# Two states to a GpSimd product, rotating pair buffers and a new table of sum slots in a selective-scan kernel

## The chip, the cores and the metric

The kernel runs on one core of a Trainium2 chip, in one launch. The metric is the device time of that launch in microseconds (us), as the median of several runs. A core has TensorE (PE, matrix products into PSUM), VectorE (DVE), ScalarE (ACT), GpSimd (POOL) and SyncE (SP, which here only issues DMA transfers). Each engine works through its own instructions in order.

## The reference, cut to what matters

The input is x of shape 16 x 192 x 64 x 64. Four layers follow each other, each of the form `x = x + layer(_gn(x))`, where `_gn` is a group norm with 32 groups. Layer 0 is a small network per channel with tanh and sigmoid, layer 1 a 1x1 convolution over five shifts of the image, layer 3 a sum of depthwise convolutions, a 1x1 convolution and a batch norm over all images. The change lies in layer 2, a selective scan in four directions k (rows, columns, and both backwards), with 16 states for each channel:

```python
def step(h, inp):
    d, u, Bt, Ct = inp
    dA = jnp.exp(d[..., None] * A)
    h = dA * h + (d * u)[..., None] * Bt[:, :, None, :]
    y = jnp.einsum('bkdn,bkn->bkd', h, Ct)
    return (h, y)
...
ys = jnp.moveaxis(ys, 0, -1) + xs * Ds.reshape(K, D)[None, :, :, None]
```

The outputs of the four directions are added in image order, and the residual adds the layer's input to that.

## The kernel before, in words

Two images are taken together: 2 x 192 channels are three tiles j of 128 partitions, and there are eight such pairs. `front` holds layers 0 and 1, the projection that gives B, C and the step sizes (`project`), and a transposition for the column directions (`split`). `scans` holds layer 2, `layer3` the last layer. The front of pair 0 runs alone; then, for each pair, `scans` runs with the front of the next pair woven in, and `layer3` follows. The last pair's `scans` has no front to weave in. The batch norm at the end closes the kernel.

In `scans` the work is 48 steps t for a pair: three tiles j, four directions k in the order 1, 3, 0, 2, and four pieces of the sequence of LC = 1024 elements. Each step has 16 states n, so there are 768 iterations s for a pair. The order of instructions on each engine is the one in which the program issues them (`E.in_order`); no scheduler changes it. One iteration s issues:

- `load_c(s+2)`: SP loads the C row of that state to all partitions (`cb`, four buffers).
- `product(s)`: DVE multiplies `du` (delta times the input) by B, in place in PSUM (`pbt`).
- `scan(s)`: DVE runs the recurrence into a buffer `h` (pool `hp`, eight buffers of LC); ACT copies the last state; POOL multiplies h by `cb`. For n = 1, 5, 9, 13, POOL also issues a transfer that adds the h of state n-1 into that of n, so of four states three are left to sum.
- `decay(s+3)`: ACT makes dA = exp(delta A).
- `spread(s+2)`: PE spreads B over the partitions with a bf16 product into one of two PSUM buffers `pbt`.
- Front work of the next pair. A credit of one unit an iteration (none at n = 5) is spent on it. A yield of layer 0 costs one unit and holds up to four 512-column f32 matmuls; a matmul of layer 1 or of the projection costs 0.57.
- `add_up(s-4)`: PE adds the h of four iterations ago to `ysum` by an identity matrix. In the places of n = 0, 4, 8, 12 `images` adds other inputs instead: for k = 0 the raw input `xc`, the normalised input through a diagonal matrix `skip`, and the sum of the column directions `Xt`; for k = 3 and k = 2 what the earlier direction left. After state 15 ACT copies ysum out.

`step_rest` makes delta and du of the next step: its matmul v (which shares the PSUM buffer of ysum) is issued at n = 4, the POOL product du at n = 10. The iteration of n = 3 issues its sum, the last of the previous step, ahead of the front work; all the others issue it behind. In layer 0, `x_rows` has SP copy the rows of a unit to the tile `m0`, ACT and PE make `t1` and `t2` from it, and `close` of the next unit adds t2 to the result. A unit is 32 rows of one chunk; a pair has 96 of them.

In the profile all instructions that `E` orders carry line L66, so they are told apart by the names of their tiles.

Of the kernel before, what the change touches and what calls it, by code (L numbers as in the profile page):

```python
# [43 lines left out]
LATE = 4  # L44
# [8 lines left out]
GAP = 25  # L53
# [53 lines left out]
def conv_preact_kernel(ctx: ExitStack, tc: tile.TileContext, a: dict):  # L107
# [43 lines left out]
    dtw = const.tile([32 + RD, K, NT, P], F32, name="t_dtw")  # L151
    for r in (0, 32):
        nc.sync.dma_start(out=dtw[r : r + RD], in_=a["dtw"])
# [11 lines left out]
    skip = const.tile([P, NT, P], F32, name="skip")  # L165
# [11 lines left out]
    for j in range(NT):  # L177
        nc.vector.tensor_scalar(skip[:, j, :], ident, dsk[:, 0, j : j + 1], None, ALU.mult)
# [126 lines left out]
    class Made:  # L305
        def __init__(self, n):
            def d(name, shape, dtype=F32):
                return dram.tile(shape, dtype, name=f"{name}{n}")

            self.x2 = d("x2_d", [NT * P, L])  # L310
            self.b = d("b_d", [P, L])
            self.c = d("c_d", [P, L])
            self.dt = d("dt_d", [K * RD, L])

            self.bp = d("bp_d", [K, BP, L], BF16)
            self.cp = d("cp_d", [2 * 2 * N, L])
            self.dtp = d("dtp_d", [2 * RD, L])
            self.gm = const.tile([P, NT], F32, name=f"gm{n}")
            self.rstd = const.tile([P, NT], F32, name=f"rstd{n}")

# [38 lines left out]
    def group_norm(E, st, stat, ps, gm, rstd, tiles=range(NT)):  # L359
# [50 lines left out]
        E.gps.tensor_tensor(rstd, d2, half, ALU.pow)  # L410


    def front(i, o, E, ps, deep):

        with tc.tile_pool(name="f_st", bufs=1) as stat:
            sts = [stat.tile([P, NT, 8, 6], F32, name=f"fst{n}") for n in range(3)]
# [35 lines left out]
            yield from layer1(o, E, ps, deep, sts[2], gms[1], rstds[1])  # L452
            yield from group_norm(E, sts[2], stat, ps, o.gm, o.rstd)
# [4 lines left out]
    def layer0(i, E, ps, deep, st, gm, rstd):  # L458
        with tc.tile_pool(name="l0w", bufs=1) as w_, tc.tile_pool(name="l0x", bufs=3) as xk, tc.tile_pool(
# [11 lines left out]
            def stream(chunks, no):  # L471
# [116 lines left out]
                for u, (ci, q) in enumerate(units):  # L588
# [13 lines left out]
                    t2 = tk.tile([GR, 2, 512], F32, name="t2", tag=f"t2{no}")  # L602
# [37 lines left out]
    def layer1(o, E, ps, deep, st, gm, rstd):  # L640
        with tc.tile_pool(name="l1w", bufs=1) as w_, tc.tile_pool(name="l1x", bufs=2) as xk, tc.tile_pool(
            name="l1r", bufs=6
# [24 lines left out]
            def load_r(c):  # L667
                if c < 8:
                    for j in range(NT):
                        xrs[c, j] = rk.tile([P, 512], F32, name="l1_xr")  # L670
                        E.sp.dma_start(
                            out=xrs[c, j], in_=row_tiles(x1_d)[:, j, 512 * c : 512 * c + 512]
                        )
# [23 lines left out]
            load_r(0)  # L697
# [4 lines left out]
            for c in range(8):  # L702
                at = 0
                for jo in range(NT):
                    p = ps("l1_p")
                    n, last = 0, 5 * len(INTO[jo]) - 1
                    for b, ji in INTO[jo]:
                        for s, (dy, dx) in enumerate(((0, 0), (0, 1), (0, -1), (1, 0), (-1, 0))):
                            E.pe.matmul(
                                p,  # L710
                                w1[:, b, s, :],
                                xps[c][:, ji, 1 + dy : 9 + dy, 1 + dx : 65 + dx],
                                start=(n == 0),
                                stop=(n == last),
                            )
                            n += 1
                            at += 1
                            if at == 4:
                                load(c + 1)
                            if at == 8:  # L720
                                load_r(c + 1)
                            if at in (15, 20, 25):
                                norm(c + 1, at // 5 - 3)
                            yield 0.57
                            advance()
                    after.append(done(c, jo, p))
# [5 lines left out]
    def project(o, E, ps):  # L732

        with tc.tile_pool(name="pjw", bufs=1) as w_, tc.tile_pool(name="pjx", bufs=3) as xk:
# [21 lines left out]
            def done(to, c, m, p):  # L756
# [4 lines left out]
                E.sp.dma_start(out=to[:, 512 * c : 512 * c + 512], in_=r)  # L761
# [34 lines left out]
    def split(o, E):  # L796

        with tc.tile_pool(name="sp1", bufs=1) as one, tc.tile_pool(name="sp2", bufs=2) as two:
            nat = one.tile([P, L], F32, name="nat")
            E.sp.dma_start(out=nat[0:64, :], in_=o.b[0:64, :])  # L800
            E.sp.dma_start(out=nat[64:128, :], in_=o.c[0:64, :])
# [19 lines left out]
            for m in range(NC_):  # L821
# [3 lines left out]
                ct = two.tile([P, LC], F32, name="ct")  # L825
# [3 lines left out]
                E.sp.dma_start(out=o.cp[:, cs], in_=ct[64:128, :])  # L829
# [23 lines left out]

    def load_dt(sp, o, k, at):
# [9 lines left out]
    def make_delta(E, v, delta, dt, k, j):  # L864

        for h in range(2):
            rows = slice(32 * h, 32 * h + RD)
            E.pe.matmul(
                v[:, 512 * h : 512 * h + 512], dtw[rows, k, j, :], dt[rows, :], start=True, stop=True
            )  # L870
# [3 lines left out]
    def load_first(o):  # L874
# [6 lines left out]
        return xn, load_bp(nc.sync, o, k, 0), dt  # L881

    def begin(o, loaded, psum):
# [3 lines left out]
        xn, bp, dt = loaded  # L887
        normalise(nc.vector, xn, xn, o.gm, o.rstd, 0)
        delta = over.tile([P, LC], F32, name="delta", tag="delta", bufs=2)
        make_delta(E, psum(), delta, dt, k, 0)  # L890
        du = over.tile([P, LC], F32, name="du", tag="du", bufs=2)
        nc.gpsimd.tensor_tensor(image(du), image(delta), columns(xn)[:, : LC // HW, :], ALU.mult)
        return xn, bp, delta, du

    def scans(i, o, p3, st3, begun, nxt):

        E = _Engines(tc, True)
        with ExitStack() as es:
# [5 lines left out]
            hp = pool("l2h", 8)  # L904
            da = pool("l2a", 3)
            cp = pool("l2c", 4)
# [5 lines left out]
            Xt = one.tile([P, L], F32, name="Xt")  # L912

# [7 lines left out]
            xns, xcs, state, bps, dts, made, ysum = {}, {}, {}, {}, {}, {}, {}  # L921
# [13 lines left out]
            def next_dt(t):  # L935
                if t < T:
                    j, k, at, first = todo[t]
                    dts[t] = load_dt(E.sp, o, k, at)

# [13 lines left out]
            def load_xc(t):  # L953
                if t < T and todo[t][1] == 0:
                    j, k, at, first = todo[t]
                    xcs[t] = one.tile([P, LC], F32, name="xc")
                    E.sp.dma_start(out=xcs[t], in_=row_tiles(o.x2)[:, j, at : at + LC])

            def load_c(s):
                t, n = divmod(s, N)  # L960
                j, k, at, first = todo[t]
                cb = cbs[s] = cp.tile([P, LC], F32, name="cb")
                src, row = (o.c, 64 + 16 * k) if k % 2 == 0 else (o.cp, 16 * (k - 1))
                for b, rows in {
# [4 lines left out]
                    r = row + N * b + n  # L969
                    E.sp.dma_start(  # L970
                        out=cb[rows, :],
                        in_=src[r : r + 1, at : at + LC].to_broadcast([rows.stop - rows.start, LC]),
                    )

            def step_rest(t):
# [5 lines left out]
                make_delta(E, v, delta, dts.pop(t), k, j)  # L981
# [28 lines left out]
            def scan(s):  # L1010
# [4 lines left out]
                dA, pbt, cb = dAs.pop(s), pbs.pop(s), cbs.pop(s)  # L1015
                back = k >= 2
                flip = slice(None, None, -1) if back else slice(None)
                h = hs[s] = hp.tile([P, LC], F32, name="h")
# [5 lines left out]
                E.gps.tensor_tensor(h, h, cb, ALU.mult)  # L1024
                if n % 4 == 1:
                    E.gps.dma_start(out=h, in_=hs[s - 1], accum_op=ALU.add)

            def add_up(s):

                t, n = divmod(s, N)  # L1030
                if s < 0:
                    return
                j, k, at, first = todo[t]
                if n % 4 == 0:
                    for c in range(LC // 512):
                        for w, v in images(t, n // 4 - 1, 512 * c):
                            E.pe.matmul(
                                ysum[t][:, 512 * c : 512 * c + 512], w, v, start=False, stop=False
                            )
                    return  # L1040
                h = hs.pop(s)
                if n % 4 == 1:
                    hs.pop(s - 1)
                if n == 1:
                    ysum[t] = py.tile([P, LC], F32, name="ysum", tag="ysum")
                for c in range(LC // 512):
                    cs = slice(512 * c, 512 * c + 512)
                    E.pe.matmul(
                        ysum[t][:, cs], ident, h[:, cs], start=(n == 1), stop=(n == N - 1)
                    )  # L1050
                if n == N - 1:
                    if k % 2:
                        E.act.copy(Xt[:, at : at + LC], ysum.pop(t))
                    else:
                        E.act.copy(rows_of(at, LC), image(ysum.pop(t)))

            def images(t, which, c):
# [3 lines left out]
                if k == 0:  # L1061
                    of = [
                        (ident, lambda: xcs[t][:, c : c + 512]),
# [9 lines left out]
                return [(w, v()) for w, v in of[which : which + 1]] if which >= 0 else []  # L1073
# [10 lines left out]
            xns[0], bps[0], *made[0] = begun  # L1084
            next_dt(1)
            for s in range(3):
                decay(s)
            for s in range(2):
                load_c(s)
                spread(s)  # L1090
            fr = front(*nxt, E, ps, False) if nxt is not None else iter(())
# [11 lines left out]
            for s in range(total):  # L1103
                t, n = divmod(s, N)
                j, k, at, first = todo[t]
                if s + 2 < total:
                    load_c(s + 2)
                if n == 2:
                    next_bp(t + 1)
                if n == 4:  # L1110
                    next_dt(t + 2)
                if n == 11:
                    load_xc(t + 1)
# [5 lines left out]
                if n == 4:  # L1119
# [8 lines left out]
                if (t + 1) % (K * NC_) == 0 and 5 <= n < 5 + NC_:  # L1128
                    norm_xn(j + 1, n - 5)
                if n > 4:  # L1130
# [3 lines left out]
                if n == 3:  # L1134
                    add_up(s - LATE)
                    if s >= LATE and todo[t - 1][1] == ORDER[-1]:
                        fin = finish(todo[t - 1][0], todo[t - 1][2] // LC)
                elif n == 10:
                    next(gstep, None)

                credit = min(credit, 0) + (n != 5)
# [3 lines left out]
                if n != 3:  # L1145
                    add_up(s - LATE)
            for s in range(total - LATE, total):
# [9 lines left out]
    def layer3(i, st3, less0, rstd0, o_next):  # L1157
        E = _Engines(tc, False)

        with tc.tile_pool(name="l3s", bufs=1) as stat, tc.tile_pool(name="l3z", bufs=2) as zk, tc.tile_pool(  # L1160
# [5 lines left out]
        ) as pz:  # L1166
            gap.tile([P, GAP * 256], F32, name="gap")
            diag = xk.tile([P, NT, PE_TAPS, P], F32, name="diag")
            xps = [xk.tile([P, S, S], F32, name=f"xp{j}") for j in range(NT - 1)] + [X]
# [278 lines left out]
```

## Time and profile before

| | |
|---|---|
| median of the runs | 27446.29 us (27440.91 to 27455.52, three runs) |
| the profiled execution | 27459.08 us, span 27457.3 us |
| mean granted TensorE clock | 0.938 |
| busy share of the span | PE 85%, DVE 87%, ACT 59%, POOL 75% |
| scans of pair 0, with a front woven in | 1202.7 to 4114.7 us: 2912.0 us |
| scans of the last pair, without a front | 23979.2 to 26746.3 us: 2767.1 us |
| layer 3 of pair 0 | 4114.7 to 4455.0 us: 340.3 us |
| C loads | 8192 DMA issues, 512 KB for each full row block |
| POOL products h*C | 6144, 2465 ns each |
| accumulating transfers | 1536, 7.4 us from issue to landing |

The span is the time from the first to the last instruction of the profiled execution. In the tables of the profile, "x" ahead of a number is a count, "idle before" is how long the engine stood idle ahead of an instruction, and the name behind "<-" is what released it. A matmul of f32 with 512 columns runs as two passes, so the records of "x4" in a timeline are two matmuls.

### The profile page before, as it was taken

Reading aid. Unit: us, or ns where it says so; the run is one execution under the profiler, and the core shown is the slowest. Engines: PE = TensorE matmul, PEld = TensorE weight load, DVE = VectorE, ACT = ScalarE, POOL = GpSimd, SP = SyncE. Lnnn points to the kernel's source line nnn. Section 1 sums busy time; section 2 is a strip of 40 time slices with the busy share of each in tenths; the row PEclk is TensorE's granted clock in tenths of the full one; section 3 lists DMA queues with packets and bytes.
Section 4 is the critical chain, followed back from the end, with each engine's and each line's share of the span. In section 5 each row is a group of like instructions: output and inputs, shape, how many; then the busy total and the mean of one; then the engine's idle time right before and its main releaser. Section 6 shows DMA issues by size and latency. Waiting matters only on the chain. (4 is left out here: it accounts for less than half of the span.)

```text
span 27457.3 us, 209986 instructions
## 1 busy us (share of the span) xinstructions
PE 23391.4 (85%) x58036; PEld 9490.8 (35%) x58036; DVE 23876.2 (87%) x15098; ACT 16298.7 (59%) x23334; POOL 20528.5 (75%) x10322
## 2 busy tenths in 40 slices
PE   8799888998789987999879988899878998766663
PEld 4343333333333332333334333333333333222221
DVE  0399998999889998999989999899989999899994
ACT  7388555874568644785447845587456864444443
POOL 2388876888778876888768887788877887677772
PEclk9899998999899998999989999999989999888886
DMA  4489874898668974898748987489856897467765
GB/s 102 132 221 226 220 226 131 224 219 218 181 182 225 222 213 142 221 224 224 218 138 220 227 219 220 138 222 218 219 173 188 225 222 215 137 190 194 202 186 245
DMA packets 2009593, 5471.86 MB, mean 199 GB/s; under 512 B 551592, under 2 KB 551816, under 8 KB 1991008
## 3 DMA queue, kind: packets, MB, share of 16 engines
q1 hardware_dynamic: 1783776, 4592.80, 57.7%
q0 software_dynamic: 221184, 805.40, 15.4%
q10 hardware_dynamic: 3456, 60.21, 0.5%
q8 instruction: 463, 7.59, 0.1%
q14 instruction: 714, 5.85, 0.1%
HBM read 3908.47 MB, written 340.96 MB: 155 GB/s over the span
## 5 line engine op out<-in xcount | busy, mean ns | idle before, releaser
L66 POOL TENSOR_TENSOR h<-h,cb 128x1024 f32<-128x1024 f32 x6144 | 14812.9, 2465 | 4331.0 <-ACT state L66 3637.1
L66 DVE TENSOR_TENSOR_SCAN h<-dA,state,pbt 128x1024 f32<-128x1024 f32 x4608 | 10807.6, 2345 | 727.0 <-ACT dA L66 119.9
L66 PE MATMUL ysum<-h,ident 128*128 128x512 f32 x18432 | 9280.1, 628 | 171.6 <-DMA h<-h 119.1
L66 DVE TENSOR_TENSOR pbt<-du,pbt 128x1024 f32<-128x1024 f32 x6144 | 7433.2, 1210 | 569.1 <-PE pbt L66 412.6
L66 ACT ACTIVATE dA<-delta,t_alog 128x1024 f32<-128x1024 f32 x6144 | 7034.6, 1146 | 6.5
L66 PEld LDWEIGHTS ysum<-h,ident 128*128 128x128 f32 x18432 | 3692.8, 202 | 4379.4 <-issue 3858.9
L66 ACT COPY state<-h 128x1 f32<-128x1 f32 x6144 | 1143.3, 186 | 6161.7 <-DVE h L66 6143.2
L66 PE MATMUL pbt<-bp,pick 96*128 96x512 bf16 x8192 | 2623.4, 404 | 1888.0 <-DVE h L66 1867.3
L66 DVE TENSOR_TENSOR_SCAN h<-dA,pbt 128x1024 f32<-128x1024 f32 x1536 | 3507.1, 2283 | 218.9 <-ACT dA L66 38.8
L66 PE MATMUL p<-t,wts 96*128 96x512 f32 x5376 | 2730.7, 605 | 162.8 <-ACT t L66 161.9
L66 PE MATMUL p<-m,wms 128*96 128x512 f32 (+1 forms) x5376 | 2662.4, 596 | 58.9 <-ACT t L66 44.7
L66 ACT ACTIVATE t<-p,bias 96x512 f32<-96x512 f32 x2688 | 1804.2, 678 | 1200.8 <-PE p L66 1187.6
L66 PEld LDWEIGHTS <-pick 96*128 96x128 bf16 x8192 | 673.7, 100 | 4795.4 <-DVE h L66 3281.0
L1209 POOL TENSOR_TENSOR l_g<-l_g,l_m 128x1024 f32<-128x1024 f32 x672 | 1627.5, 2423 | 620.9 <-ACT l_g L1205 474.7
L66 PE MATMUL l_p<-l_xp,w1s 128*128 128x512 f32 x3920 | 1883.3, 596 | 0.0
L66 PE MATMUL pbt<-bp,pick_mix 96*128 96x512 bf16 x4096 | 1270.1, 392 | 560.0 <-DVE h L66 555.5
L66 POOL DMA_DIRECT2D h<-h x1536 | 1356.3, 883 | 495.4 <-POOL h L66 419.3
L66 PEld LDWEIGHTS p<-t,wts 96*128 96x128 f32 x5376 | 1012.1, 191 | 1323.2 <-issue 883.4
L66 ACT ACT_TABLE_LOAD x1082 | 1388.2, 1283 | 19.0
L66 PEld LDWEIGHTS p<-m,wms 128*96 128x96 f32 (+1 forms) x5376 | 941.0, 177 | 811.8 <-issue 355.7
L1232 DVE SCALAR_TENSOR_TENSOR l_p<-xp,wc,l_p 128x1024 f32<-128x1024 f32 x768 | 990.4, 1290 | 223.8 <-PE l_p L1226 198.1
L66 ACT ACTIVATE m<-m,bias,sp 96x512 f32<-96x512 f32 x1344 | 1077.6, 802 | 87.0 <-DMA m<-l_xn 85.1
(241 smaller groups left out, 18647.7 us busy)
## 6 DMA issues: line engine op xcount, KB each, us to landing
cb<-cp_d SPq DMA_DIRECT2D x2048, 512.0 KB
cb<-c_d SPq DMA_DIRECT2D x2048, 512.0 KB
h<-h POOLq DMA_DIRECT2D x1536, 512.0 KB, 7.4
cb<-cp_d SPq DMA_DIRECT2D x2048, 256.0 KB
cb<-c_d SPq DMA_DIRECT2D x2048, 256.0 KB
m<-l_xn SPq DMA_DIRECT2D x3072, 128.0 KB
bp<-bp_d SPq DMA_DIRECT2D x384, 192.0 KB
rl<-x_d ACTq DMA_DIRECT2D x24, 2450.0 KB
```

The costliest lines, as they stand in the source:

```text
L66: return self._tc.keep_in_program_order(call(*args, **kw))
L1209: nc.gpsimd.tensor_tensor(g, g, m, ALU.add)
L1232: nc.vector.scalar_tensor_tensor(image(y if tap is TAPS[-1] else ps), window(j, 16 * c, 16, tap), factor(j, tap), image(ps), ALU.mult, ALU ...
```

## The change

- The h buffers hold two states each (2 x LC, five buffers that rotate, so ten states). POOL makes one product of 2 x LC elements after the odd state. Of the transfer that adds one state of four nothing changes but its place in the pair buffer.
- C is stored so that two states' rows lie one behind the other, and one load brings two (three buffers of 2 x LC).
- `xc` with its load and its matmul goes. As the raw input is std times the normalised one plus the mean, `skip` becomes a diagonal matrix of the D sum plus std, made once a pair, and the mean is the bias of ACT's copy of ysum for k = 0.
- The sums get a table: `AFTER` has the iterations after a step's start at which something is added, `SUMS` the state (or, negative, the image) that is added there. The first is state 1 in iteration 8, the last state 15 in iteration 22, which is n = 6 of the next step; this one is issued ahead of the front work.
- In turn other steps move: `step_rest` to n = 7 and its du to n = 11, `next_dt` and the iteration without credit to n = 8, `norm_xn` to n = 4, 5, 8, 9, `finish` to n > 7.
- `dtw` is loaded for each j and k rather than kept. In layer 0 `t2` is written into `m0`. Layer 1's `l1r` pool has five buffers for six, and loads its three rows one at a time. The statistics tiles `fst` are two for three, `ct` in `split` is single. In layer 3 the tile `xp1` moves into the pool of the gap, which shrinks.

```diff
-LATE = 4
+AFTER = (8, 10, 11, 12, 13, 14, 15, 16, 17, 18, 19, 20, 21, 22)
+SUMS = (1, 2, 3, 5, 6, 7, -1, 9, 10, 11, -2, 13, 14, 15)
+WHEN = {slot - AFTER[0]: what for slot, what in zip(AFTER, SUMS)}
...
+        if std is not None:
+            E.gps.tensor_tensor(std, d2, rstd, ALU.mult)
...
-                    t2 = tk.tile([GR, 2, 512], F32, name="t2", tag=f"t2{no}")
+                    t2 = m0[:GR]
...
-            name="l1r", bufs=6
+            name="l1r", bufs=5
...
-            hp = pool("l2h", 8)
+            hp = pool("l2h", 5)
-            cp = pool("l2c", 4)
+            cp = pool("l2c", 3)
...
-                cb = cbs[s] = cp.tile([P, LC], F32, name="cb")
+                cb = cbs[u] = cp.tile([P, 2 * LC], F32, name="cb")
...
+                    two = src[at // LC, r : r + 2, :].rearrange("r l -> (r l)").unsqueeze(0)
                     E.sp.dma_start(
-                        out=cb[rows, :],
-                        in_=src[r : r + 1, at : at + LC].to_broadcast([rows.stop - rows.start, LC]),
+                        out=cb[rows, :], in_=two.to_broadcast([rows.stop - rows.start, 2 * LC])
                     )
...
-                h = hs[s] = hp.tile([P, LC], F32, name="h")
+                u, of = divmod(s, 2)
+                if of == 0:
+                    hs[u] = hp.tile([P, 2 * LC], F32, name="h")
+                h = hs[u][:, LC * of : LC * of + LC]
...
-                E.gps.tensor_tensor(h, h, cb, ALU.mult)
-                if n % 4 == 1:
-                    E.gps.dma_start(out=h, in_=hs[s - 1], accum_op=ALU.add)
+                if of:
+                    E.gps.tensor_tensor(hs[u], hs[u], cbs.pop(u), ALU.mult)
+                    if u % 2 == 0:
+                        E.gps.dma_start(
+                            out=hs[u][:, LC:], in_=hs[u][:, :LC], accum_op=ALU.add
+                        )
...
+                    u, of = divmod(N * t + what, 2)
+                    h = hs[u][:, LC * of + 512 * c : LC * of + 512 * c + 512]
                     E.pe.matmul(
-                        ysum[t][:, cs], ident, h[:, cs], start=(n == 1), stop=(n == N - 1)
+                        ysum[t][:, cs], ident, h, start=(what == 1), stop=(what == N - 1)
                     )
...
+                    elif k == 0:
+                        E.act.activation(
+                            rows_of(at, LC),
+                            image(ysum.pop(t)),
+                            AF.Identity,
+                            bias=o.gm[:, j : j + 1],
+                        )
...
                     of = [
-                        (ident, lambda: xcs[t][:, c : c + 512]),
                         (skip[:, j, :], lambda: xns[j][:, at : at + 512]),
                         (ident, lambda: columns(Xt)[:, at // HW : at // HW + 8, :]),
                     ]
...
+            E.gps.tensor_tensor(gain, dsk[:, 0, :], o.std, ALU.add)
+            for j in range(NT):
+                E.act.activation(skip[:, j, :], ident, AF.Copy, scale=gain[:, j : j + 1])
...
-                if s + 2 < total:
-                    load_c(s + 2)
+                if s % 2 == 0 and s + 2 < total:
+                    load_c(s // 2 + 1)
...
-                if n == 4:
+                if n == 7:
                     gstep = step_rest(t + 1) if t + 1 < T else iter(())
                     next(gstep, None)
...
-                if n == 3:
-                    add_up(s - LATE)
-                    if s >= LATE and todo[t - 1][1] == ORDER[-1]:
+                if n == 6:
+                    add_up(s)
+                    if t and todo[t - 1][1] == ORDER[-1]:
                         fin = finish(todo[t - 1][0], todo[t - 1][2] // LC)
-                elif n == 10:
+                elif n == 11:
                     next(gstep, None)
 
-                credit = min(credit, 0) + (n != 5)
+                credit = min(credit, 0) + (n != 8)
...
-                if n != 3:
-                    add_up(s - LATE)
+                if n != 6:
+                    add_up(s)
```

## The prediction

> **What bounds the kernel now.** I read the busy shares first, then the busy time by stage, the waits of VectorE (DVE), and last the timeline of two engines over three iterations.
>
> The page's head (engine, busy us, share of the span, instructions):
>
> ```profile
> span 27457.3 us, 209986 instructions
> PE 23391.4 (85%) x58036; PEld 9490.8 (35%) x58036; DVE 23876.2 (87%) x15098; ACT 16298.7 (59%) x23334; POOL 20528.5 (75%) x10322
> L66 POOL TENSOR_TENSOR h<-h,cb 128x1024 f32<-128x1024 f32 x6144 | 14812.9, 2465 | 4331.0 <-ACT state L66 3637.1
> ```
>
> DVE is busiest, PE close behind, and no share says which ends last. The table by stage (us of the stage, then busy us of PE, PEld, DVE, ACT, POOL; PE clock) has the scans of the first two pairs and of the last, which has no front woven in:
>
> ```profile
> 1202.70:4114.70 2912.00, 2613.23 (x6590) 1063.40 (x6591) 2731.59 (x1668) 1898.81 (x2792) 2353.18 (x1200) 0.96 0.84 224
> 4455.00:7363.00 2908.00, 2610.14 (x6592) 1063.18 (x6592) 2731.30 (x1669) 1901.06 (x2793) 2352.23 (x1200) 0.96 0.85 224
> 23979.20:26746.30 2767.10, 1891.95 (x4267) 694.26 (x4268) 2665.40 (x1564) 1200.03 (x1752) 2092.42 (x1012) 0.86 0.71 195
> ```
>
> DVE idles 2912.00 - 2731.59 = 180.4 and 176.7 us with a front, 2767.10 - 2665.40 = 101.7 without. The last is its small pause between instructions (101.7/768 = 0.13 us an iteration), so at most 178.5 - 101.7 = **76.8 us a pair** can be won in each of the seven pairs with a front. VectorE's waits (us in total, times, longest) say what those are:
>
> ```profile
> DVE pbt L66 <- PE pbt L66: 412.6, 553, 4.2
> DVE h L66 <- ACT dA L66: 158.7, 491, 2.7
> DVE h L66 <- DMA h<-h: 137.6, 90, 5.9
> ```
>
> 412.6/7 = 59 a pair for PE, 158.7/8 = 20 for the decays, 137.6/7 = 20 for the accumulating transfers; no scan waits on PE for the buffer of an h. The timeline of PE and of DVE (start, us, operation):
>
> ```profile
> 5597.25 0.60 PE L66 MATMUL pbt<-bp,pick_mix 96*128 96x512 bf16 x2
> 5597.68 1.02 PE L66 MATMUL p<-m,wms 128*128 128x512 f32 x2
> 5598.54 1.02 PE L66 MATMUL p<-t,wts 96*128 96x512 f32 x2
> 5599.40 1.88 PE L66 MATMUL ysum<-h,ident 128*128 128x512 f32 x4
> 5601.12 0.60 PE L66 MATMUL pbt<-bp,pick_mix 96*128 96x512 bf16 x2
> 5603.72 0.61 PE L66 MATMUL pbt<-bp,pick_mix 96*128 96x512 bf16 x2 [0.29 <-DVE h L66]
> ```
> ```profile
> 5601.31 2.35 DVE L66 TENSOR_TENSOR_SCAN h<-dA,state,pbt 128x1024 f32<-128x1024 f32 x1
> 5603.58 1.21 DVE L66 TENSOR_TENSOR pbt<-du,pbt 128x1024 f32<-128x1024 f32 x1
> 5604.89 2.35 DVE L66 TENSOR_TENSOR_SCAN h<-dA,state,pbt 128x1024 f32<-128x1024 f32 x1
> ```
>
> DVE repeats every 5604.89 - 5601.31 = 3.58 us. One PE iteration with front and sum takes 5601.12 - 5597.25 = 3.87: spread 0.43, front 1.72, sum 1.72. The scan shown ending at 5601.31 + 2.35 = 5603.66 releases spread at 5603.72 (0.06 later); the next scan starts 1.23 after that end.
>
> **The new slots and buffers.** Five rotating pairs hold ten states. The scan of state n, n even, overwrites the pair of ten states earlier. For state 12 that is the pair of 2 and 3, and the new table sums state 3 in slot 11: in PE's written order behind spread(13) and the front work of iteration 11. Spread(13) cannot start before scan 11 has ended, since pbt has two PSUM buffers. So scan 12 hangs on a chain that starts at the end of scan 11: 0.06 + (0.43 + 1.72 + 1.72, and 0.16 that a last pass is shown longer, which is 5599.40 + 1.88 - 5597.25 = 4.03) + about 0.04 to start = 4.13 us, where 1.23 was enough. **Stall: 2.90 us** a step. Queued behind it on DVE are all later products, and ACT and POOL follow the scans. Without front work the chain is 0.06 + 0.43 + 1.88 + 0.04 = 2.41, a stall of 1.18. Layer 1 and project charge 0.57 credit a matmul, so 1.75 of 0.86 us, 1.51 for the 1.72: 2.69.
>
> Steps by kind: layer 0 yields 96 units x 4 at 15 a step, 25.6 steps; layer 1 (280 x 0.57) and project (72 x 0.57), 13.3; 9.1 of 48 have none. A pair: 25.6 x 2.90 + 13.3 x 2.69 + 9.1 x 1.18 = **120.7 us**. Nothing hides it: DVE has no other work at that place.
>
> The other even scans (0, 2, 4, 6, 10, 14) now wait for the sum of iteration n - 2, where before only the product waited for a spread two iterations old. PE's slack falls from 3.58 - 0.06 - 0.43 = 3.1 us to (1.23 + 3.58) - 4.13 = 0.7, while layer 0 iterations with a sum cost PE 0.3 more than DVE. Bounds a pair: 0 (the stall at state 12 lets PE catch up each step) and today's 59; I take 28, in between.
>
> **PE's clock.** Released by the sum, scan 12 runs while PE waits for it: 2.4 us idle a step. Such a gap in the trace of before:
>
> ```profile
> 11868.09 0.91 PE L66 MATMUL pbt<-bp,pick 96*128 96x512 bf16 x2 [2.00 <-DMA m<-l_xn]
> 11868.79 3.32 PE L66 MATMUL p<-m,wms 128*96 128x512 f32 x4
> 11871.95 1.88 PE L66 MATMUL ysum<-h,ident 128*128 128x512 f32 x4
> ```
>
> Spread and front took 11871.95 - 11868.09 = 3.86 instead of 2.15: half rate, 1.71 lost. Of the 28 gaps of 2.0 to 2.6 us that I found inside dense stretches, 18 (65%) were followed by half-rate passes. Scan 14 waits for that iteration's sum with 0.7 of slack, so 0.65 x (1.71 - 0.7) x 39 steps = 25 us a pair; bounds 0 and 39 us. In the last pair the clock is low 27% of the time already, and the spread and sum of the chain cost 2.15 more then: 0.27 x 2.15 = 0.58 a step, taken for the 9.1 front-less steps of the others too (5.3 us).
>
> The Trainium skill, "TensorE: Matmul & The Clock Gate", Part 1 (The HAM clock gate), lets the array go cold after an idle window of about 3.4 us, so gaps of 2.4 us would cost nothing; by it the sum below would be 25 x 7 lower, some 175 us. The rows above disagree, and I go by them.
>
> **What is removed.** POOL: two products of 2465 ns become one of twice the size. Queued ones follow each other at 2465, so 4.9 us at most, and 4.4 if a fixed part of about half a us is saved; 8 x 4.9 + 4 transfers x 0.88 + du 3.1 = 46 us of a 57 us step. POOL is not the bound: worth 0 on the path. It starts only after the odd scan, but state sums come seven iterations (25 us) later instead of four; a transfer lands in 7.4 us (median), so the 20 us a pair for transfers go. C loads: half as many on SP, same bytes, issued two iterations ahead; 0 while three buffers cover it, at worst what the transfers cost today, 20. The xc matmuls: 1.72 us on 12 k = 0 steps, which need PE 6.9 + 20.6 + 25.8 + 1.7 + 5.2 = 60.2 us (16 spreads, 12 sums, 15 of front, v, three images) against DVE's 16 x 3.58 = 57.3; now 58.5. This, and slots at 7 iterations, removes most of the 59 us of PE waits, already counted as gone. The gain matrix is one POOL and three small ACT instructions a pair: hidden behind DVE's first products, 2 us if not. The mean rides as bias in a copy that exists.
>
> **What is added besides.** dtw comes in two small DMAs on SP per j, k, four steps ahead of use in iteration 7: nothing, or up to 1 us x 12 a pair. Fewer l1r, fst and ct buffers spread their loads: nothing seen waits on them; at most some us. xp1 in the gap pool waits for the last sums, but its first use is behind the 46 us of POOL sums in layer 3: nothing. The drain after the last scan holds two more iterations of sums: +2 us x 8 = 16. t2 in m0: SP's row loads wait for PE's closing adds, with later C loads queued behind; 0 if rows still land within the three iterations that they have, at worst 1 us for each of 96 units; I take 0, the nearest row being that ACT waits 85 us in all for these rows today.
>
> **The sum.** Each front pair: 120.7 + 28 + 25 + 5.3 + 20 (decays, kept) = 199, for 76.8 today: +122.2, x 7 = +855. Last pair: 48 x (1.18 + 0.58) = +84. Drain +16. The profiled execution took 27459.08 (span 27457.3 and 1.8 around it): 27459 + 955 = 28414. It lay 13 us above the median of 27446.29, so **28400 us**. About 0.2% (55 us) is what a measurement of this kernel can tell from no change.
>
> **Rivals.**
> (1) Faster: slot 11 does not hold scan 12 back (a release by halves, or front-work too sparse there) and the old waits go: -(76.8 - 20) x 7 + 16 = -382, so 27064. It decides if the added wait is below 382/384 = 1.0 us for each of the 384 steps. For: PE waits and DMA waits fall indeed. Against: even the front-less chain costs 1.18. 6%.
> (2) Slower, but the stall swallows every other wait (lag, decays, clock): (120.7 - 76.8) x 7 + 48 x 1.18 + 16 = +380, 27826. For: each step starts with PE caught up. 20%.
> (3) t2's reuse delays the rows: 1 us x 96 x 7 = +672 on top, 29072. For: SP now waits behind PE, which itself runs late. Against: three iterations of cover. 12%.
> The forecast keeps 62%; its own bounds (lag 0 to 59, clock 0 to 39) move it by -370 and +310. The range 27830 to 28850 reaches from rival 2 to a third of rival 3 added to high lag. Faster by over 0.2%: 0.06; within: 0.02; slower: 0.92.
>
> **What would show it.** In the profile after: about 384 waits of scans for PE ysum, at state 12, of 2.9 us (1.2 to 1.8 in the last pair), over 900 us in all; PE idle about 2.4 us right after each; waits for DMA h<-h gone and those for PE pbt well below 412.6; POOL h<-h,cb x3072 at 4.4 to 4.9 us; DVE busy the same within 1%. It is wrong if scans wait for PE under 400 us in all, if the waits sit at other states, or if ACT waits for m<-l_xn rows have grown by hundreds of us.

## The result and the profile after

The changed kernel took 28849.34 us (28836.44 to 28851.26, four runs) against 27445.3 us: a ratio of 1.051, 95% interval 1.0492 to 1.0528. That is inside the range of the prediction by 0.7 us and 449 us above its number: the added time was 1404 us, not 955. The direction and the main mechanism were right; other terms were mis-sized, and that their sum stayed inside the range is luck.

The head of the page after, and the POOL and DVE groups that changed (columns as before; the line of all that `E` orders is L68 here):

```profile
span 28848.0 us, 197960 instructions
PE 23657.3 (82%) x57652; PEld 9635.6 (33%) x57652; DVE 23821.0 (83%) x15095; ACT 16351.1 (57%) x23358; POOL 20025.1 (69%) x7266
L68 POOL TENSOR_TENSOR h<-h,cb 128x2048 f32<-128x2048 f32 x3072 | 13972.0, 4549 | 5944.1 <-ACT state L68 5621.6
L68 DVE TENSOR_TENSOR_SCAN h<-dA,state,pbt 128x1024 f32<-128x1024 f32 x4608 | 10808.2, 2346 | 2140.8 <-PE ysum L68 1606.5
```

DVE does the same work in the same time (23821.0 us busy, 23876.2 before), every engine's share falls, and the span grows: a new wait. The scan's own line names it, 1606.5 us ahead of the scans, for PE's sums. The stages, in the columns of the table before (pairs 0 and 1, and the last pair):

```profile
1205.80:4305.40 3099.60, 2641.40 (x6536) 1078.63 (x6537) 2722.81 (x1668) 1907.85 (x2794) 2290.40 (x818) 0.95 0.80 208
4640.70:7739.40 3098.70, 2640.01 (x6536) 1078.26 (x6537) 2722.88 (x1669) 1908.84 (x2797) 2290.22 (x818) 0.95 0.80 208
25258.70:28133.50 2874.80, 1904.99 (x4212) 718.24 (x4213) 2665.28 (x1564) 1202.39 (x1755) 2021.36 (x629) 0.86 0.73 184
```

A pair with a front costs 187 us more on the mean of the seven (1308 in all), the last pair 107.7. The seven layer 3 stages are 32 us shorter together (pair 0: 340.3 to 335.3); prologue and tail add 6. The sum, 1390, is the difference of the spans, 1391, but for 1 us. DVE's waits (us in total, times, longest):

```profile
DVE h L68 <- PE ysum L68: 2053.2, 1015, 10.1
DVE h L68 <- ACT dA L68: 208.8, 673, 2.6
DVE pbt L68 <- PE pbt L68: 49.0, 54, 2.9
```

The waits for spreads (412.6) and for transfers (137.6) are nearly gone, as forecast, and a wait of 2053.2 us stands in their place. Sorted by state n, 1416.9 us of it lie ahead of scan 12, in 379 of its 384 executions; the other 636 lie ahead of the other even scans. One of them, on PE and on DVE:

```profile
5535.74 0.60 PE L68 MATMUL pbt<-bp,pick 96*128 96x512 bf16 x2
5536.18 1.88 PE L68 MATMUL p<-m,wts 96*128 96x512 f32 x4
5537.90 1.88 PE L68 MATMUL ysum<-h,ident 128*128 128x512 f32 x4
5542.39 0.59 PE L68 MATMUL pbt<-bp,pick 96*128 96x512 bf16 x2 [2.60 <-DVE h L68]
```
```profile
5535.60 1.21 DVE L68 TENSOR_TENSOR pbt<-du,pbt 128x1024 f32<-128x1024 f32 x1
5539.98 2.35 DVE L68 TENSOR_TENSOR_SCAN h<-dA,state,pbt 128x1024 f32<-128x1024 f32 x1 [3.18 <-PE ysum L68]
5542.25 1.21 DVE L68 TENSOR_TENSOR pbt<-du,pbt 128x1024 f32<-128x1024 f32 x1
```

Read it in the order of release: scan 11 ends (the product at 5535.60 follows it), PE does spread, front and sum back to back until 5537.90 + 1.88 = 5539.78, scan 12 starts at 5539.98 after 3.18 us of nothing, and PE then idles 2.60 us until scan 12 has ended. Each side waits for the other once a step.

### The profile page after: what moved, and what is told of

It reads as the page before. It is cut to its first block, busy times and chain, and to the rows that moved or that the text cites. A ratio compares the mean times of both kernels' runs of the same rounds, so it can differ in the third digit from the quotient of the medians.

```text
span 28848.0 us, 197960 instructions
## 1 busy us (share of the span) xinstructions
PE 23657.3 (82%) x57652; PEld 9635.6 (33%) x57652; DVE 23821.0 (83%) x15095; ACT 16351.1 (57%) x23358; POOL 20025.1 (69%) x7266
## 4 chain that ended last, share of the span: by engine, by line
PE 41%; DVE 33%; ACT 12%; POOL 6%; issue 5%; DMA 2%; DVEq 0%; SPq 0%; POOLq 0%; ACTq 0%
DVE h L68 23%; PE ysum L68 17%; PE p L68 11%; DVE pbt L68 8%; POOL l_g L1233 4%; PE pbt L68 4%; ACT dA L68 4%; PE l_p L1238 2%; PE l_p L68 2%; ACT L68 2%; PE pj_p L68 1%; ACT m L68 1%; POOL h L68 1%; PE p L511 1%; PE l_p L708 1%
## 5 line engine op out<-in xcount | busy, mean ns | idle before, releaser
L68 POOL TENSOR_TENSOR h<-h,cb 128x2048 f32<-128x2048 f32 x3072 | 13972.0, 4549 | 5944.1 <-ACT state L68 5621.6
L68 DVE TENSOR_TENSOR_SCAN h<-dA,state,pbt 128x1024 f32<-128x1024 f32 x4608 | 10808.2, 2346 | 2140.8 <-PE ysum L68 1606.5
L68 PE MATMUL ysum<-h,ident 128*128 128x512 f32 x18432 | 9397.7, 635 | 49.4 <-issue 41.0
L68 DVE TENSOR_TENSOR pbt<-du,pbt 128x1024 f32<-128x1024 f32 x6144 | 7418.6, 1207 | 192.2 <-POOL du L903 140.9
L68 ACT ACTIVATE dA<-delta,t_alog 128x1024 f32<-128x1024 f32 x6144 | 7034.1, 1146 | 6.5
L68 ACT COPY state<-h 128x1 f32<-128x1 f32 x6144 | 1146.5, 187 | 7432.1 <-DVE h L68 7409.4
L68 PEld LDWEIGHTS ysum<-h,ident 128*128 128x128 f32 x18432 | 3751.1, 205 | 4361.5 <-issue 4093.0
L68 PE MATMUL pbt<-bp,pick 96*128 96x512 bf16 x8192 | 2638.2, 405 | 2585.2 <-DVE h L68 2573.2
L68 DVE TENSOR_TENSOR_SCAN h<-dA,pbt 128x1024 f32<-128x1024 f32 x1536 | 3507.9, 2284 | 658.2 <-PE ysum L68 446.7
L68 PE MATMUL p<-m,wms 128*96 128x512 f32 (+1 forms) x5376 | 2732.2, 610 | 99.2 <-ACT lu L68 56.7
L68 PEld LDWEIGHTS <-pick 96*128 96x128 bf16 x8192 | 748.5, 101 | 5483.3 <-issue 3850.1
L68 PE MATMUL pbt<-bp,pick_mix 96*128 96x512 bf16 x4096 | 1281.9, 395 | 1005.8 <-DVE h L68 990.6
L68 PE MATMUL l_p<-l_xp,w1s 128*128 128x512 f32 x3920 | 1943.9, 613 | 0.0
L68 POOL DMA_DIRECT2D h<-h x1536 | 1356.8, 883 | 495.0 <-POOL h L68 463.3
L68 PE MATMUL p<-m,wts 96*128 96x512 f32 x2688 | 1381.3, 630 | 163.8 <-ACT m L68 163.7
L68 PE MATMUL p<-t,wts 96*128 96x512 f32 x2688 | 1391.5, 598 | 0.0
L68 ACT ACTIVATE m<-p,bias 96x512 f32<-96x512 f32 x1344 | 909.7, 677 | 768.9 <-PE p L68 767.2
L68 PEld LDWEIGHTS p<-m,wms 128*96 128x96 f32 (+1 forms) x5376 | 949.4, 179 | 886.4 <-issue 385.1
L68 ACT ACTIVATE t<-p,bias 96x512 f32<-96x512 f32 x1344 | 900.8, 681 | 513.4 <-PE p L68 501.8
```

The costliest lines, as they stand in the source:

```text
L68: return self._tc.keep_in_program_order(call(*args, **kw))
```

## The experiments

All ratios are to the kernel before, timed beside the runs of the same batch.

**1. The place of the wait.** One line moves the sums of states 2 and 3 a slot forward:

```diff
-AFTER = (8, 10, 11, 12, 13, 14, 15, 16, 17, 18, 19, 20, 21, 22)
+AFTER = (8, 9, 10, 12, 13, 14, 15, 16, 17, 18, 19, 20, 21, 22)
```

> The changed kernel with the sums of states 2 and 3 one slot earlier (9 and 10). The theory, that scan 12 waits for the sum of slot 11, makes scan 12 as loose as scan 14: its mean gap falls from 3.95 us (front pairs) and 2.25 us (last pair) to about 0.72 and 0.24, which is (3.23 x 7 + 2.01) x 48 = 1180 us less than 28849: 27670, with some 100 us more if PE, no longer pausing there, carries its lateness into the other even scans. The rival, that PE itself is the bound in these steps and the place of the wait is chance, lets the waits reappear at scans 14, 0, 2, 4 and gains less than half of that: above 28250.

Measured: 27659.03 us, ratio 1.0074 (1.0059 to 1.0089). 1190 of the 1404 us go with one tuple entry of each of two sums. The gap ahead of scan 12 fell from a mean of 3.95 us to 0.64 in the pairs with a front, from 2.25 to 0.13 in the last; the gaps of the other even scans stayed within 0.15 us of what they were, so nothing reappeared elsewhere. DVE's waits for sums and for spreads in this run:

```profile
DVE h L68 <- PE ysum L68: 704.1, 666, 6.2
DVE pbt L68 <- PE pbt L68: 78.2, 87, 3.4
```

The loss at scan 12 is the wait for slot 11, and the rival, that PE's lateness would show up at other scans, is out.

**2. What the front work has to do with it.** The sum of iteration 11 is issued ahead of that iteration's front work, everything else as in the changed kernel:

```diff
+                if n == 11:
+                    add_up(s)
                 if n == 6:
                     add_up(s)
...
-                if n != 6:
+                if n not in (6, 11):
                     add_up(s)
```

> The changed kernel with the sum of iteration 11 issued ahead of that iteration's front work. The theory takes the front passes (3.5 of 0.43 us on average in the trace, 44 of 48 steps) out of the chain to scan 12: 1.5 x 44 x 7 = 460 us less, about 28390; the wait at scan 12 falls from 3.95 to about 2.6 us in the front pairs and stays at 2.25 in the last. The rival, that the wait is PE's general lateness, gives less than 100 us, as the same matmuls run in the same iteration.

Measured: 28149.31 us, ratio 1.0253 (1.0238 to 1.0268): 700 us less, not 460. At scan 12 the gap fell by 1.59 us (3.95 to 2.36), which is 534 us over 48 steps of seven pairs, close to what was expected. The rest came at scan 14 (0.72 to 0.36) and scans 0 and 2. The front work now lies in PE's forced pause after the sum, so PE should start the next iterations earlier. Also, pauses of 2.0 to 2.7 us after scan 12 fell from 331 to 62 in the seven pairs, and the granted clock of these stages rose from 0.946 to 0.959. The run does not part these two.

**3. More slack for all even scans.** Every sum but that of state 1 one slot earlier, the last at n = 5:

```diff
-AFTER = (8, 10, 11, 12, 13, 14, 15, 16, 17, 18, 19, 20, 21, 22)
+AFTER = (8, 9, 10, 11, 12, 13, 14, 15, 16, 17, 18, 19, 20, 21)
...
-                if n == 6:
+                if n == 5:
                     add_up(s)
...
-                if n != 6:
+                if n != 5:
                     add_up(s)
```

> The changed kernel with every sum but state 1's one slot earlier (slots 8 to 21 without a gap; the last at n = 5, ahead of the front work). The theory frees scan 12 as in the run with states 2 and 3 alone (27670) and gives scans 0, 2, 4, 6 and 14 a whole iteration more; their gaps above the usual 0.1 us add up to 2.0 us a step, 2.0 x 48 x 7 = 670 us: down to 27000 to 27250. The rival: six iterations are too short for the accumulating transfer (8.5 us to landing, behind POOL's 4.55 us product), so PE waits for transfers at the sums of states 5, 9 and 13 and the gain over the other run is under 200 us.

Measured: 27457.87 us, ratio 1.0002 (0.9993 to 1.0012): 201 us less than experiment 1, not the 400 to 650 of the theory. It is not the rival either, since PE waited only 28 us for transfers at its sums. DVE's waits tell:

```profile
DVE pbt L68 <- PE pbt L68: 394.3, 456, 5.4
DVE h L68 <- ACT dA L68: 205.7, 527, 3.0
DVE h L68 <- PE ysum L68: 171.1, 96, 6.2
```

The waits for sums went from 704.1 to 171.1, and those for spreads came back from 78.2 to 394.3, about where they were before the change (412.6). My reading is that PE is about as late as before once the buffers are out of the way, and that the buffers had only met that lateness first. It is not a like for like: this version has less PE work (experiment 4) and rows that come later (experiment 5; ACT waits 291.9 us for them here).

**4. One part alone: x and skip as one image,** in the kernel before. The lines are those of the change; the core of them:

```diff
-                        (ident, lambda: xcs[t][:, c : c + 512]),
                         (skip[:, j, :], lambda: xns[j][:, at : at + 512]),
...
+            for j in range(NT):
+                E.act.activation(skip[:, j, :], ident, AF.Copy, scale=gain[:, j : j + 1])
```

> The kernel before with one part of the change alone: x and skip as one image. It takes 1.72 us of PE from 12 steps of each pair that need 60.2 us of PE against 57.3 of DVE. The theory: where the woven front fills PE (about half of these steps) the time comes off, up to 1.72 x 6 x 7 = 72 us, so about 27375 to 27420. The rival: the lateness is absorbed by the iterations without front or sum in any case, and nothing over 25 us is seen.

Measured: 27354.16 us, ratio 0.9962 (0.9948 to 0.9976). 102 us less than the 27456.25 beside it, more than the 72 expected at most and so outside the theory's range, while the rival is out. DVE's waits for spreads fell by 80 us (412.6 to 332.3) and those for transfers by 18 (137.6 to 119.6).

**5. A second part on top: t2 in m0.**

```diff
-                    t2 = tk.tile([GR, 2, 512], F32, name="t2", tag=f"t2{no}")
+                    t2 = m0[:GR]
```

> The kernel before with x and skip as one image and t2 written into m0: a second part of the change on top of the first, against 27354 for the first alone. The theory that t2's reuse costs nothing (the prediction's value) gives 27330 to 27380. The rival, that SP's row loads and the C loads behind them now wait for PE's closing adds and the rows come late to ACT (in the run with all slots earlier ACT waited 292 us for them, 85 in the kernel before), gives 27450 to 27600, with ACT's waits for the rows above 200 us.

Measured: 27439.75 us, ratio 0.9989 (0.998 to 0.9998), 86 us above experiment 4, or 76 when each is compared with the kernel before timed beside it (27456 and 27466). That lies between the two ranges, 10 us short of the rival's. The line of SP's queue that shows it, in experiment 4 and here (the first fence is without, the second with t2 in m0), and what ACT waits for rows here:

```profile
SPq L66 <- PE p L66: 438.8, 306, 5.3
```
```profile
SPq L66 <- PE p L66: 2352.9, 559, 9.9
```
```profile
ACT m L66 <- DMA m<-l_xn: 227.6, 134, 5.8
```

SP now stands behind PE's closing adds, and ACT waits 227.6 us for rows against 74.2 in experiment 4. The theory that it costs nothing falls, and the sign that the rival named, over 200 us of ACT's waits, is there. In the changed kernel SP waited 5234.8 us for PE there, but ACT's waits for rows grew only from 85.1 to 105.2 us.

**6. Six pair buffers,** with two C buffers instead of three, as there was no room for both:

```diff
-            hp = pool("l2h", 5)
+            hp = pool("l2h", 6)
...
-            cp = pool("l2c", 3)
+            cp = pool("l2c", 2)
```

> The changed kernel with its own slots, but six pair buffers for h, and to make room two instead of three for C. The theory, that the whole loss is the wait for buffers, gives every even scan two iterations more: waits of scans for sums below 100 us in all, time 27350 to 27480 (what the run with all slots earlier reached, or less). The rival: with two C buffers POOL's products wait for their C loads, and the accumulating transfers behind them come late for the sums: above 27600.

Measured: 28137.44 us, ratio 1.0243 (1.0228 to 1.0259). No wait of a scan for a sum was left, but the time was above 27600, as the rival said, though not by its way: POOL's waits for C loads rose from 176.8 to 632.0 us, but PE's sums hardly waited for transfers. PE's, SP's and ACT's waits:

```profile
PE ysum L68 <- DMA h<-h: 0.5, 1, 0.5
```
```profile
SPq L68 <- POOL h L68: 13892.2, 2669, 12.4
```
```profile
ACT m L68 <- DMA m<-l_xn: 1199.3, 329, 11.7
```

SP stands in its C loads until POOL frees a buffer (13892.2 us, 7513.1 in the changed kernel), and the rows of layer 0 wait behind them in the same queue: 1199.3 us at ACT. Of ACT's 330 waits for rows, 295 follow within 20 us a C load that stood over 2 us in SP's queue; in the changed kernel 8 of 54. The total alone does not tell: in the kernel before SP stands 10292.5 us in this line and ACT waits 85.1. PE's front matmuls wait for ACT (475.8 us, 163.7 in the changed kernel), and DVE's products 1119.4 us for PE's spreads.

**7. t2 in its own tile again in the version of experiment 3,** also with two C buffers for room:

```diff
-                    t2 = m0[:GR]
+                    t2 = tk.tile([GR, 2, 512], F32, name="t2", tag=f"t2{no}")
...
-            cp = pool("l2c", 3)
+            cp = pool("l2c", 2)
```

> The run with all slots earlier (27458), with t2 in a tile of its own again, and two C buffers to make room. If t2's reuse is what holds that version above the 27354 of the one image alone, it falls to 27330 to 27400 and ACT's waits for the rows fall from 292 us towards 85. If it is not, it stays at 27440 to 27480, or rises if two C buffers are too few.

Measured: 28038.56 us, ratio 1.0207 (1.0191 to 1.0222). ACT waited 1111.9 us for rows, as in experiment 6, although t2 had its own tile. So two C buffers alone delay the rows, and the run says nothing of t2 in that version; what t2 costs there stays open. Only experiment 5 measures t2, in the kernel before.

**8. A ninth h buffer** for experiment 4, in the room of xc:

```diff
-            hp = pool("l2h", 8)
+            hp = pool("l2h", 9)
```

> The kernel before with x and skip as one image and a ninth h buffer (in the room that xc leaves). The theory: the 120 us that scans wait for accumulating transfers come from taking back a buffer 3.6 us too early; one more buffer removes most of it, 27250 to 27290. The rival: the transfers are late in any case and PE's sums meet them instead; above 27330.

Measured: 27323.09 us, ratio 0.9948 (0.9932 to 0.9965); the interval overlaps that of experiment 4, so the two cannot be told apart for sure. The time missed the theory's range by 33 us and stayed just under the rival's. The waits of scans for transfers fell from 119.6 to 11.9 us as the theory said, those of PE's sums for them did not rise (122.4 to 100.6), and those for spreads rose from 332.3 to 389.5. So about half of the wait that went, 57 of 108 us, came back as a wait for PE.

**9 and 10. Less PE work where PE is the bound.** In both versions a second iteration without front work, in the 19 steps of layer 0 in each pair that also add an image; first in experiment 3, then in experiment 8:

```diff
-                credit = min(credit, 0) + (n != 8)
+                credit = min(credit, 0) + (n != 8 and not (n == 10 and k != 1 and t < 27))
```
```diff
-                credit = min(credit, 0) + (n != 5)
+                credit = min(credit, 0) + (n != 5 and not (n == 13 and k != 1 and t < 27))
```

> The run with all slots earlier (27458), with no front work at n = 10 either in the 19 layer 0 steps that also add an image (k = 3, 0, 2). If what still holds it up is PE, which has more to do in those steps than DVE, this takes 1.72 us off each of them and takes the front out of the chain to scan 12: its waits for sums at scan 12 (136 us) go and those for spreads fall below 250 us, time 27150 to 27300. If instead the rows that come late through SP (t2 in m0) hold it, PE waits as long for ACT and the gain is under 80 us.

Measured: 27392.37 us, ratio 0.9972 (0.9963 to 0.9982). A gain of 65 us: the waits for sums fell to 42.8, but those for spreads stayed (412.3), and ACT still waits 327.2 us for rows. By the time and by these waits that is the alternative, but the run does not settle it. In the profiled executions of experiments 3 and 9 the scans of the seven front pairs, from the first scan's start to the last one's end, took 20444 and 20276 us: 168 less, a gain of the theory's size. The layer 3 stages between the pairs took 2352 and 2437, 85 more, for a reason that stays open; behind pair 0 ACT normalises layer 3's input after its last copy of ysum here, ahead of it in experiment 3.

> The kernel before with one image and nine h buffers (27323), with no front work at n = 13 in the same 19 steps of a pair. PE's waits for spreads, 390 us, fall by up to 1.72 x 19 x 7 = 229 us: 27100 to 27200, the fastest of all. If they come from ACT's or the rows' lateness instead, nothing over 60 us.

Measured: 27118.07 us, ratio 0.9877 (0.9861 to 0.9894), the fastest of all, 1.2% below the kernel before and 6% below the changed one, in the theory's range; lateness of ACT or the rows is out as the main cause here. The waits for spreads fell by 85 us only, though (389.5 to 304.4), of a gain of 205; the rest was not traced to one wait. DVE's wait, and a pair with a front:

```profile
DVE pbt L66 <- PE pbt L66: 304.4, 314, 7.5
```
```profile
4405.60:7267.80 2862.20, 2580.65 (x6543) 1051.26 (x6544) 2726.43 (x1669) 1898.25 (x2787) 2355.91 (x1202) 0.97 0.85 224
```

2862.20 us against 2908.00: DVE idles 135.8 us, of which the last pair shows some 100 to be its small pauses.

## Why the prediction was right, and where its steps were off

- **The slot-11 chain: right, shown by experiment 1.** Worked out as 4.07 us from spread to scan plus 0.06; in the layer 0 steps of the trace its median was 4.24 (a layer 0 yield holds at most two matmuls, four passes, which is the 1.72 us in it). The prediction's price of the chain with the clock lost behind it was (120.7 + 25 + 5.3) x 7 + 84 = 1141 us; taking the chain away gave 1190. That these agree so well is partly luck. Scan 12 alone lost 159 us a pair by the chain (3.95 - 0.64 us in 48 steps), where 120.7 + 5.3 were forecast; the clock term of 25 at scan 14, where only 7 went with the chain, made up for part of the difference. What the sum had at nothing is that PE was not on time when scan 11 ended but 1.3 us late on average in layer 0 and 0.7 in the later front steps. The front reached into step 43, not 39 (the yields without matmuls were not counted; the trace of before has it at 43 too). At steps 9 and 25 of each pair ACT's table loads (ACT_TABLE_LOAD in the profile) fall between scans 11 and 12: PE waits for ACT inside the chain, and scan 12 is held up by 9.7 us in step 9 of pair 0. Steps 8, 15 and 24 of pair 0 are held up 7.6 to 8.8 us without a table load there.
- **The other even scans: the term that was furthest off.** I set them at 28 us a pair with bounds of 0 and 59; their gaps rose by about 90. The upper bound was the wait for spreads in the trace of before, which had 3.1 us of slack behind it. With 0.7 us of slack the same lateness is met oftener, so that was no bound. Experiment 3 gave them an iteration more and their waits were gone but for 35 us at scan 10, whose slot had not moved.
- **The removed waits counted as gained.** The sum took 76.8 - 20 = 56.8 us a pair off. The waits for spreads and transfers did fall, by 52 and 20 us a pair, but most of the first not for the reason given. In experiment 3, with looser slots, the waits for spreads were back at 394.3 us, so in the changed kernel the scans had met PE's lateness first: what was taken off for spreads stood again ahead of the even scans. What left for good with PE's xc matmul was 102 us in all (experiment 4). Of the missing 449 us, the even scans are about 430 (62 x 7) and scan 12 about 230 (184 us a pair more than before, for 120.7 + 25 + 5.3, x 7); smaller differences took the rest back.
- **t2 in m0: taken as 0, worth 76 to 86 us in the kernel before** (experiment 5). I had named the mechanism as rival 3 and priced it at up to 672; the size was between. In the changed kernel itself ACT's waits for rows rose by only 20 us, so the sign that I had named, hundreds of us, did not show; that the stalls there give the rows time is likely but not shown.
- **PE's clock: too large.** After 113 of 331 pauses of 2.0 to 2.7 us behind scan 12 in the pairs with a front (34%, not 65%), at least half a us was lost in the spread and front work that followed, 1.4 us each on average. Counted in the same way, 13 of all 64 such pauses (2.0 to 2.6 us) in the front pairs of the kernel before lost that much; the prediction's 28 were picked in dense stretches. The Trainium skill, "TensorE: Matmul & The Clock Gate", Part 1 (The HAM clock gate), would have none by its idle window of about 3.4 us; the trace lies between the two.
- **POOL and the C loads: right, worth nothing.** The paired product took 4549 ns, in the range given, and saved POOL 840.9 us of busy time, for which no run shows a gain. All that the pairs, the C loads, the new slots and the smaller buffer changes together add to experiment 5 is 27458 - 27440 = 18 us in the loosest version (28 against the kernel before beside each); none of them was run alone.
- **The rivals.** The first is out: the wait binds in 379 of 384 steps. The second had the stall swallow the other waits of scans; the waits for spreads did go, but those ahead of the other even scans came and were longer. The third is a real mechanism, but small, as above.
- **The drain: not seen.** I added 16 us; the layer 3 stages, in which it lies, became 4.5 us shorter a pair. No run shows what the drain alone costs.

The runs form a chain from the kernel before to the changed one: before 27456; one image -102; t2 in m0 +86; pairs, C loads and slots at their loosest +18; one slot less slack +201; slot 11 +1190. That this makes 28849 is so by construction, as each step is the difference of two neighbours (t2 was timed beside a kernel before of 27466, so 10 us may belong to the next step). Only the last two come from where the sums lie.

## What to carry to other kernels

When buffers are rotated rather than freed, write down for every reuse which instruction releases it and what stands before that instruction in its engine's queue. A release queued behind something that waits for the iteration just ended turned two engines that ran side by side into a chain here, which no busy share showed. A wait that a change removes may come back as a wait for the next engine that is late; here only the versions that took matmuls from PE, or moved them out of the crowded steps, ran faster than the kernel before.

## What the runs showed of the hardware

One product of 2048 elements a partition took 4549 ns on POOL where two of 1024 took 2 x 2465, a saving of 381 ns a pair by these durations and 274 by POOL's busy time (840.9 us in 3072 products), as the shorter records overlap. The accumulating transfer took 8.5 us to land after the change and 7.4 before, with the same bytes. With two C buffers it took 9.5 and 9.6. SP's order was the surprise: with two C buffers, loads that waited for a buffer held up the row loads behind them, and ACT waited 1199.3 and 1111.9 us for rows (experiments 6 and 7).
